# Blocks of many and of few columns by turns, in a three-layer graph attention kernel

## The chip, the cores and the metric

The kernel runs on one core of a Trainium2 chip. The metric is the device time of one execution in microseconds; before the change it is 3365.79 us, the median of three runs (3364.47 to 3366.1). A core has five engines with queues of their own: PE (matrix products), DVE (vector work), ACT (functions and scaling), POOL (here above all the issue of gathers) and SP (plain transfers).

## The reference

There are 6250 nodes with 256 features and 100,000 edges, sorted by destination. Two graph attention layers of 4 heads with 64 features (each with loops from a node to itself) are followed by one of 8 heads with 32 features, with layer normalisation after the second and the third.

```python
# layers 1 and 2 (GATv2): per edge and head
xl = x @ Wl; xr = x @ Wr
logits = sum(leaky_relu(xl[src] + xr[dst], 0.2) * att)      # over a head's features
alpha = exp(logits - max over dst) / sum over dst
out = segment_sum(xl[src] * alpha, dst) + b
# layer 3 (GAT): the logit is a sum of two numbers per node and head
e = leaky_relu(s1[src] + s2[dst], 0.2)
out = segment_sum(softmax over dst (e) * Wh[src], dst)

h = elu(layer1(x)); x = layernorm(x + layer2(h)); x = layernorm(x + layer3(x))
```

Each layer needs, for each node, the rows of all nodes that point to it. A node has 16 such sources on average, some have over 30 and some under 5.

## The kernel before

A planning part (`make_plan`) counts the edges of every node, ranks the nodes by that number, and puts them into 49 blocks of 128, one node to a partition. Block 0 has the nodes with the most edges, block 48 those with the fewest. `columns` gives each block a number of columns, the most edges a node in it may have: 27 in block 0 (edges over that are handled apart, in the `few_...` helpers), then 25, 24, 23, 22, 21, 21, 20, ... down to 10, 10 and 9 in the last ones; 803 in all. While the plan is made the table of layer 1 (rows of x Wl, one to a node) is written to device memory.

`tile_by_degree` then runs the three layers over the blocks, in the order of an instruction stream written out by hand (nothing is rescheduled). For a block with c columns, POOL issues c indirect gathers (L1235), each of which brings one row of about 1 KB to each of the 128 partitions. They go to row tiles of up to 9 rows (`row_tiles`, `chunks`): a block of 28 slots (27 columns and, in layers 1 and 2, the node's own row) takes 4 tiles, 19 to 27 slots take 3, 10 to 18 take 2. There are 9 row tiles, used in turn (`rowp`, L1201); a gather waits until the tile's last user is done.

Layers 1 and 2 are in `layer2`. In iteration b the streams are: POOL `start(b + 3)` (layer 1 only: one gather of the nodes' lists and features) and `gather(b + 1)`; PE and ACT `ready(b + 1)`, the node's own products (layer 1) or copies (layer 2); `attend(b)`: on DVE three passes over each tile (maximum, product with att, sum; L1504 to L1506) for the logits, their maximum (`top`, L1374), on ACT the exponentials (L1381); then `end(b - 1)`, which scales and finishes the block before; DVE's reciprocal of the sum (L1571, called den here, which waits for the exponentials); and `weighted_sum(b)`: DVE multiplies the rows by their weights (L1411), ACT does so for the last few columns (L1410), and PE adds the rows up in PSUM by products with the identity (L1418). Last, the finished row of block b - 1 is transposed (L1355), copied by ACT (xT, L1357), multiplied by the next layer's weights (L1362) and stored by SP: the next layer's table. The block order of PE and ACT is fixed: the transposes of b - 1 stand behind the sums of b, and the exponentials of b + 1 behind the copies of b - 1.

Layer 3 has no products on PE: DVE adds the logits (L1703), weights the rows (L1433) and sums them (L1442); POOL scatters finished rows to the output (L1733).

A layer's gathers need the whole table of the layer before. To begin earlier, `begin` gathers the first columns of the first three blocks (14, 12 and 11, `EARLY`) out of the rows of blocks 0 to 44 only; it stands in POOL's stream behind the last block's gathers. For that, `sort_sources` sorts those blocks' sources in layer 1 (DVE, in `attend` of the following block), so that the early ones lie in these rows.

Of the kernel before, what the change touches and what calls it, by code (L numbers as in the profile page):

```python
# [26 lines left out]
F32 = mybir.dt.float32  # L27
BF16 = mybir.dt.bfloat16
I32 = mybir.dt.int32
AF = mybir.ActivationFunctionType  # L30
OP = mybir.AluOpType
# [4 lines left out]
P = 128  # L36
# [2 lines left out]
EPS = 1e-5  # L39
FAR = 1 << 20  # L40
RUNS = 64
EARLY = (14, 12, 11)
LATE = 4


def columns(E, N, NB):

    mean = E / N
    pmf = [math.exp(-mean)]
    for k in range(1, 200):
        pmf.append(pmf[-1] * mean / k)
    over, sd = [], []
    for c in range(199):
        p = sum(pmf[c + 1 :])
        g = sum((k - mean) * pmf[k] for k in range(c + 1, 200))
        over.append(N * p)  # L60
        sd.append(math.sqrt(max(N * (p * (1.0 - p) - g * g / mean), 0.0)))
    cols = []
    for b in range(NB):
        most = P * b
        cols.append(next(
            c for c in range(199) if (over[c] + 3.5 * sd[c] <= most if b else over[c] < 0.01)
        ))
    low = max((c for c in range(199) if N - over[c] <= P // 4), default=0)
    high = next(c for c in range(199) if over[c] <= P // 4)
    pmf += [0.0] * 200  # L70
    held = next(
        c for c in range(199)
        if N * sum((k - c) * pmf[k] for k in range(c, 200))
        + 3.5 * math.sqrt(N * sum((k - c) ** 2 * pmf[k] for k in range(c, 200))) <= P
    )
    assert cols[1] <= held < cols[0]
    return cols, low, high, held


@with_exitstack  # L80
# [634 lines left out]
def make_plan(  # L715
# [6 lines left out]
    nc = tc.nc  # L722
    N, F = x.shape
    E = src.shape[0]
    NB = node_i.shape[1]
# [12 lines left out]
    one = ctx.enter_context(tc.tile_pool(name="plan_one", bufs=1))  # L738
# [4 lines left out]
    ps = ctx.enter_context(tc.tile_pool(name="plan_ps", bufs=1, space=PSUM))  # L743
# [301 lines left out]
    place_f = one.tile([P, NB], F32, name="place_f")  # L1045
# [3 lines left out]
    piece = one.tile([P, 2, NB], I32, name="piece")  # L1049
    nc.vector.tensor_single_scalar(piece[:, 0, :], place, P - 1, op=OP.bitwise_and)  # L1050
    nc.vector.tensor_single_scalar(piece[:, 1, :], place, 7, op=OP.logical_shift_right)
    nc.vector.tensor_scalar(vals[:, 2, :], count, 255.0, None, op0=OP.min)
    to = one.tile([P, 2, NB], BF16, name="to")
    nc.vector.tensor_copy(to, piece)
# [56 lines left out]
    pb = ps.tile([P, 2], F32, name="pb", tag="ph")  # L1111
# [31 lines left out]
def tile_by_degree(  # L1143
# [3 lines left out]
    nc = tc.nc  # L1147
# [3 lines left out]
    NB = -(-N // P)  # L1151
# [8 lines left out]
    consts = ctx.enter_context(tc.tile_pool(name="deg_consts", bufs=1))  # L1160
# [13 lines left out]
    spots = sources  # L1174


    AHEAD = (NB - LATE) * P
# [16 lines left out]
    lack = consts.tile([P, FEW], F32, name="few_lack")  # L1194
    few_at = consts.tile([P, 2], I32, name="few_at")
    few_row = consts.tile([P, max(W2 + 1, A1)], F32, name="few_row")
    soon = consts.tile([P, len(EARLY), max(EARLY)], I32, name="soon")
    late = consts.tile([P, len(EARLY)], F32, name="late")
    ones = consts.tile([P, P], F32, name="ones_l")
    nc.gpsimd.memset(ones, 1.0)  # L1200
# [29 lines left out]
    def gather_rows(b, rows, cut, own, table, of, width, j0, j1):  # L1230


        for g, (s0, s1) in zip(rows, cut):
            for j in range(max(s0 - own, j0), min(s1 - own, j1)):
                nc.gpsimd.indirect_dma_start(  # L1235
                    out=g[:, j + own - s0, :width], out_offset=None, in_=table,
                    in_offset=source(of, b, j),
                )
# [74 lines left out]
    def row_tiles(b, own):  # L1313
        cut = chunks(cols[b] + own)
        return [rowp.tile([P, T, RW], F32, name="g") for _ in cut], cut

    def begin(own, table, width):

        for b, n in enumerate(EARLY):
            begun[b] = row_tiles(b, own)  # L1320
            gather_rows(b, *begun[b], own, table[:AHEAD], soon, width, 0, n)

    def sort_sources(work, ps, b):

        n = cols[b]
        keys = work.tile([P, CK], F32, name="keys")
        nc.vector.memset(keys, -float(NP << KEY))
        nc.vector.tensor_single_scalar(
            keys[:, :n], spots[:, b, :n], -float(1 << KEY), op=OP.mult
        )  # L1330
        nc.vector.tensor_sub(keys, keys, number)
        order = work.tile([P, CK], F32, name="order")
        for r in range(0, CK, 8):
            nc.vector.max(order[:, r : r + 8], keys)
            if r + 8 < CK:
                nc.vector.match_replace(keys, order[:, r : r + 8], keys, -BIG)
        places = work.tile([P, CK], I32, name="places")
        nc.vector.tensor_single_scalar(places, order, -1.0, op=OP.mult)
        nc.vector.tensor_single_scalar(spots[:, b, :n], places[:, :n], KEY, op=OP.logical_shift_right)
        e = EARLY[b]  # L1340
        nc.vector.tensor_single_scalar(soon[:, b, :e], spots[:, b, :e], AHEAD - 1, op=OP.min)
        nc.vector.tensor_single_scalar(
            late[:, b : b + 1], spots[:, b, e - 1 : e], float(AHEAD), op=OP.is_ge
        )
        if b + 1 == len(EARLY):
            pb = ps.tile([P, b + 1], F32, name="pb", tag="tp")
            nc.tensor.matmul(pb, ones, late, start=True, stop=True)
            bad = work.tile([P, 1], F32, name="bad")
            nc.vector.reduce_sum(bad, pb, axis=AX.X)
            nc.vector.tensor_single_scalar(done, bad, 0.0, op=OP.is_equal)  # L1350
# [115 lines left out]
    def layer2(i, table, of, width, start, own, finish, follow):  # L1466
# [5 lines left out]
        with ExitStack() as es:  # L1472
            zp = es.enter_context(tc.tile_pool(name=f"z{i}", bufs=1))
            work = es.enter_context(tc.tile_pool(name=f"work{i}", bufs=3))
            ps = es.enter_context(tc.tile_pool(name=f"ps{i}", bufs=2, space=PSUM))
# [6 lines left out]
            def gather(b):  # L1482
                first = EARLY[b] if b in begun else 0
                rows, cut = begun.pop(b) if first else row_tiles(b, 1)
                gather_rows(b, rows, cut, 1, table, of, width, first, cols[b])
                if b == 0:
                    gather_few(table, i, width)
                state[b] = [rows, cut]
# [8 lines left out]
            def attend(b):  # L1497
                rows, cut, xr = state.pop(b)
                S = cols[b] + 1
                lg = work.tile([P, CM + 1, H2], F32, name="lg")  # L1500
                for g, (s0, s1) in zip(rows, cut):
                    n = s1 - s0
                    z = zp.tile([P, T, W2], F32, name="z")[:, :n, :]
                    nc.vector.tensor_max(z, g[:, :n, :W2], xr[:, None, :].to_broadcast([P, n, W2]))  # L1504
                    nc.vector.tensor_mul(z, z, at[:, None, :].to_broadcast([P, n, W2]))  # L1505
                    nc.vector.reduce_sum(  # L1506
                        lg[:, s0:s1, :], z.rearrange("p t (h d) -> p t h d", h=H2), axis=AX.X
                    )
                if b == 0:
                    own_r = work.tile([P, W2], F32, name="few_own", bufs=1)  # L1510
                    nc.scalar.copy(own_r, xr)
                    po = pst.tile([P, W2], F32, name="few_r", tag="tp")
                    nc.tensor.matmul(po, node_of, own_r, start=True, stop=True)
                    none(po)
                    z = zp.tile([P, T, W2], F32, name="z")[:, 0, :]
                    nc.vector.tensor_max(z, few_row[:, :W2], po)
                    nc.vector.tensor_mul(z, z, at)
                    few_lg = work.tile([P, H2], F32, name="few_lg", bufs=1)
                    nc.vector.reduce_sum(few_lg, per_head(z, H2), axis=AX.X)
                    few_logits(work, pst, lg, few_lg, H2)  # L1520
                    if i == 0:
                        nc.vector.tensor_copy(few_at[:, 1:], few_row[:, W2 : W2 + 1])
                few = min(S // 3, cut[-1][1] - cut[-1][0] - 1) if b + 1 < NB else 0
                wt, new = weights(work, ps, lg, S if b else S + FEW, H2, few, S)
                while later:
                    later.pop()()
                if i == 0:
                    for g, (s0, s1) in zip(rows, cut):
                        s = max(s0, 1)
                        nc.scalar.copy(spots[:, b, s - 1 : s1 - 1], g[:, s - s0 : s1 - s0, W2])  # L1530
                    if 0 < b <= len(EARLY):
                        sort_sources(work, pst, b - 1)
                return rows, cut, wt, new

# [55 lines left out]
    def none(t):  # L1590

        nc.vector.memset(t.rearrange("p (h d) -> p h d", h=H2)[:, :, D2:], -BIG)
# [86 lines left out]
    with ExitStack() as es:  # L1679
        work = es.enter_context(tc.tile_pool(name="work3", bufs=3))  # L1680
        ps = es.enter_context(tc.tile_pool(name="ps3", bufs=3, space=PSUM))
# [111 lines left out]
```

## Time and profile before

| | us |
|---|---|
| median of the runs | 3365.79 |
| profiled execution | 3880.55 |
| its span, first to last instruction | 3878.7 |
| DVE busy | 2836.2 |
| POOL busy | 2530.5 |
| PE busy | 1481.8 |
| ACT busy | 1091.1 |

The profiled execution is 515 us longer than the runs. Busy times are added up over the whole program; the layers have different limits, so they are read by stretch. The gathers of layer 1 begin at 154.5 us, those of layer 2 that need all rows at 1512.4, those of layer 3 at 2722.4. A POOL gather counts as busy while it is issued (0.95 us), not until its rows have landed. Idle time in a group's line stands ahead of its instructions, with what ended it.

### The profile page before, as it was taken

To read this page: it belongs to the slowest core of one execution; us is meant where nothing else is said; L and a number is where in the kernel's file an instruction comes from. 1 tells how busy PE (TensorE), PEld (TensorE's weight loads), DVE (VectorE), ACT (ScalarE), POOL (GpSimd) and SP (SyncE) were. 2 spreads that over 40 slices of the span, in tenths; PEclk is the share of its full clock that TensorE was granted. 3 is DMA by queue.
4 is the path that set the end of the run, shared out by engine and by line. 5 is a ranking of instruction groups with operands and counts; after the bars stand their busy time and mean duration, and the time that the engine had idled before them with its cause. 6 is when DMAs were issued, how large, how long until landed. Compare 5 with 4: busy or idle time off the path is not lost.

```text
span 3878.7 us, 23608 instructions
## 1 busy us (share of the span) xinstructions
PE 1481.8 (38%) x5130; PEld 1113.8 (29%) x5130; DVE 2836.2 (73%) x2648; ACT 1091.1 (28%) x4176; POOL 2530.5 (65%) x2613
## 2 busy tenths in 40 slices
PE   6324665556667763355544545554000000000000
PEld 5213444434555542343433433443000000000000
DVE  6228988668888876899876988896676565666665
ACT  3113444334445442243433434443000000000000
POOL 6464666666666645666666666664777777777774
PEclk8656877778788886676666677776555555555555
DMA  8532333333434334333433434442343333333332
GB/s 188 109 92 78 98 104 104 100 99 103 105 102 108 104 79 109 100 106 104 112 107 105 111 107 110 109 111 74 101 108 101 96 97 96 97 97 96 97 97 57
DMA packets 196123, 395.60 MB, mean 102 GB/s; under 512 B 63036, under 2 KB 115514, under 8 KB 195956
## 3 DMA queue, kind: packets, MB, share of 16 engines
q0 software_dynamic: 122048, 338.04, 33.2%
q1 hardware_dynamic: 66226, 54.22, 5.1%
q10 hardware_dynamic: 7698, 1.74, 0.4%
q8 instruction: 45, 0.74, 0.1%
q14 instruction: 106, 0.87, 0.1%
HBM read 353.82 MB, written 40.42 MB: 102 GB/s over the span
## 4 chain that ended last, share of the span: by engine, by line
issue 20%; POOL 20%; DVE 13%; PE 10%; another core or an unknown queue 6%; ACT 5%; DMA 1%; DVEq 0%; POOLq 0%; ACTq 0%
POOL g L1235 18%; PE acc L1418 6%; DVE z L1505 4%; DVE z L1504 4%; DVE lg L1506 3%; PE pm L1362 3%; ACT g L1410 2%; ACT wt L1381 2%; DVE g L1411 1%; POOL out L1733 1%; DMA g<-xl_d,near_r 1%; DVE weighted L1433 1%; ACT xT L1357 0%; PE pt L1355 0%
## 5 line engine op out<-in xcount | busy, mean ns | idle before, releaser
L1235 POOL DMA_INDIRECT g<-xl_d,near_r x1569 | 1487.4, 948 | 858.7 <-issue 454.3
L1418 PE MATMUL acc<-g,ident 128*128 128x256 f32 x3408 | 1015.9, 461 | 765.3 <-issue 282.7
L1418 PEld LDWEIGHTS acc<-g,ident 128*128 128x128 f32 x3408 | 774.4, 234 | 1004.2 <-issue 522.3
L1235 POOL DMA_INDIRECT g<-whs_d,near_r x766 | 793.2, 1036 | 284.2 <-issue 250.0
L1410 ACT ACTIVATE g<-g,by 128x64 f32<-128x64 f32 x2056 | 545.1, 337 | 316.1 <-issue 310.8
L1504 DVE TENSOR_TENSOR z<-g,pr 128x1820 f32<-128x1820 f32 (+4 forms) x234 | 497.1, 2125 | 19.1 <-DMA g<-xl_d,near_r 10.0
L1505 DVE TENSOR_TENSOR z<-z,at 128x1820 f32<-128x1820 f32 (+4 forms) x234 | 497.4, 2126 | 8.0
L1506 DVE TENSOR_REDUCE lg<-z 128x28 f32<-128x1820 f32 (+4 forms) x234 | 497.3, 2125 | 8.1
L1442 DVE TENSOR_REDUCE acc_v<-weighted 128x256 f32<-128x4096 f32 (+15 forms) x49 | 343.7, 7014 | 16.5 <-remote 8.3
L1411 DVE TENSOR_TENSOR g<-g,wt 128x1792 f32<-128x1792 f32 (+8 forms) x234 | 348.4, 1505 | 2.9
L1391 ACT ACTIVATE wt<-lg 128x128 f32<-128x128 f32 (+17 forms) x49 | 14.0, 285 | 851.0 <-DVE top L1374 391.5
L1703 DVE TENSOR_TENSOR lg<-g,s_r 128x56 f32<-128x56 f32 (+4 forms) x111 | 22.1, 213 | 315.1 <-DMA g<-whs_d,near_r 272.5
L1357 ACT COPY xT<-pt 128x256 f32<-128x256 f32 x147 | 54.9, 374 | 688.5 <-remote 342.2
L1433 DVE TENSOR_TENSOR weighted<-g,wt 128x1792 f32<-128x1792 f32 (+4 forms) x111 | 226.6, 2056 | 0.1
L1571 DVE RECIPROCAL den<-den 128x4 f32<-128x4 f32 x98 | 17.4, 177 | 212.9 <-ACT wt L1381 165.2
L1381 ACT ACTIVATE wt<-lg,top 128x19 f32<-128x19 f32 (+14 forms) x392 | 116.0, 296 | 190.8 <-DVE lg L1506 74.3
L1362 PE MATMUL pm<-wcat,xT 128*128 128x260 f32 x392 | 136.0, 505 | 56.3 <-ACT xT L1357 49.8
L1362 PE MATMUL pm<-wh_cat,xT 128*128 128x272 f32 x196 | 77.5, 531 | 183.8 <-ACT xT L1357 95.5
L1537 DVE TENSOR_TENSOR h<-acc,den 128x256 f32<-128x256 f32 x98 | 40.7, 416 | 126.2 <-remote 112.8
L1362 PEld LDWEIGHTS pm<-wcat,xT 128*128 128x128 f32 x392 | 94.8, 255 | 90.5 <-ACT xT L1357 64.6
L1362 PEld LDWEIGHTS pm<-wh_cat,xT 128*128 128x128 f32 x196 | 42.8, 242 | 203.0 <-ACT xT L1357 104.7
L1362 PE MATMUL pl<-wcat,xT 128*128 128x260 f32 x196 | 64.0, 455 | 55.5 <-issue 40.4
(232 smaller groups left out, 1548.4 us busy)
## 6 DMA issues: line engine op xcount, KB each, us to landing
g<-xl_d,near_r POOLq DMA_INDIRECT x1569
g<-whs_d,near_r POOLq DMA_INDIRECT x766
whs_d<-row SPq DMA_DIRECT2D x49, 132.0 KB
xl_d<-xl SPq DMA_DIRECT2D x49, 130.0 KB
xl_d<-row SPq DMA_DIRECT2D x49, 130.0 KB
xr_d<-row SPq DMA_DIRECT2D x49, 130.0 KB
two<-xl_d SPq DMA_DIRECT2D x49, 130.0 KB
two<-xr_d SPq DMA_DIRECT2D x49, 130.0 KB
```

The lines of the kernel that those rows point to most:

```text
L1235: nc.gpsimd.indirect_dma_start(out=g[:, j + own - s0, :width], out_offset=None, in_=table, in_offset=source(of, b, j),)
L1357: nc.scalar.copy(xT, pt)
L1362: nc.tensor.matmul(pm, xT[:, c, :], w[:, c, :], start=c == 0, stop=c == 1)
L1381: nc.scalar.activation(wt[:, :, h], lg[:, :S, h], AF.Exp, bias=top[:, h : h + 1], accum_out=den[:, h : h + 1],)
L1410: nc.scalar.mul(g4[:, t, h, :], g4[:, t, h, :], by[:, t - m, h : h + 1])
L1411: nc.vector.tensor_mul(g4[:, :m], g4[:, :m], wt[:, s0 : s0 + m, :].unsqueeze(3).to_broadcast([P, m, H, F // H]),)
L1418: nc.tensor.matmul(acc, ident, g4[:, t], start=s0 + t == 0, stop=s0 + t == S - 1 and not more)
L1433: nc.vector.tensor_mul(prod[:, s0 - base : s1 - base, :].rearrange("p t (h d) -> p t h d", h=H), g[:, :n, :F].rearrange("p t (h d) -> p t ...
L1442: nc.vector.reduce_sum(part, prod[:, : s1 - base, :].rearrange("p s f -> p f s"), axis=AX.X)
L1504: nc.vector.tensor_max(z, g[:, :n, :W2], xr[:, None, :].to_broadcast([P, n, W2]))
L1505: nc.vector.tensor_mul(z, z, at[:, None, :].to_broadcast([P, n, W2]))
L1506: nc.vector.reduce_sum(lg[:, s0:s1, :], z.rearrange("p t (h d) -> p t h d", h=H2), axis=AX.X)
```

## The change

The numbers of columns are dealt out by turns: block 0 keeps 27, block 1 gets the fewest (9), block 2 the next most (25), block 3 the next fewest (10), and so on, so that the sizes meet in the end: ..., 17, 15, 17, 15, 16, 16, 16, 16, 16. The same nodes stay together; only the place of a block changes. The plan computes the place from the rank in three small DVE instructions and rebuilds the number written to the table in a fourth, so tables, lists and output follow the new order in all three layers. The early gathers are 14 columns of block 0 and 12 of block 2, now the two largest, and only those two are sorted. Numbers of gathers, tiles and bytes stay as they were.

```diff
-EARLY = (14, 12, 11)
+EARLY = {0: 14, 2: 12}
...
     assert cols[1] <= held < cols[0]
-    return cols, low, high, held
+    turns = [0] * NB
+    for r, c in enumerate(cols):
+        turns[min(2 * r, 2 * NB - 1 - 2 * r)] = c
+    return turns, low, high, held
...
     nc.vector.tensor_single_scalar(piece[:, 1, :], place, 7, op=OP.logical_shift_right)
+    back = one.tile([P, NB], I32, name="back")
+    nc.vector.tensor_scalar(
+        back, piece[:, 1, :], -2.0, float(2 * NB - 1), op0=OP.mult, op1=OP.add
+    )
+    nc.vector.tensor_single_scalar(piece[:, 1, :], piece[:, 1, :], 2.0, op=OP.mult)
+    nc.vector.tensor_tensor(piece[:, 1, :], piece[:, 1, :], back, op=OP.min)
+    nc.vector.scalar_tensor_tensor(
+        place_f, piece[:, 1, :], float(P), piece[:, 0, :], op0=OP.mult, op1=OP.add
+    )
...
-        for b, n in enumerate(EARLY):
+        for b, n in EARLY.items():
             begun[b] = row_tiles(b, own)
             gather_rows(b, *begun[b], own, table[:AHEAD], soon, width, 0, n)
...
-        e = EARLY[b]
+        e, k = EARLY[b], list(EARLY).index(b)
...
-        if b + 1 == len(EARLY):
-            pb = ps.tile([P, b + 1], F32, name="pb", tag="tp")
+        if b == max(EARLY):
+            pb = ps.tile([P, k + 1], F32, name="pb", tag="tp")
...
-                    if 0 < b <= len(EARLY):
+                    if b - 1 in EARLY:
                         sort_sources(work, pst, b - 1)
```

More of the change, by code (lines that the diff above doesn't have):

```diff
@@ L1196, in tile_by_degree @@
     few_row = consts.tile([P, max(W2 + 1, A1)], F32, name="few_row")
-    soon = consts.tile([P, len(EARLY), max(EARLY)], I32, name="soon")
+    soon = consts.tile([P, 1 + max(EARLY), max(EARLY.values())], I32, name="soon")
     late = consts.tile([P, len(EARLY)], F32, name="late")
@@ L1339, in sort_sources @@
         nc.vector.tensor_single_scalar(spots[:, b, :n], places[:, :n], KEY, op=OP.logical_shift_right)
-        e = EARLY[b]
+        e, k = EARLY[b], list(EARLY).index(b)
         nc.vector.tensor_single_scalar(soon[:, b, :e], spots[:, b, :e], AHEAD - 1, op=OP.min)
         nc.vector.tensor_single_scalar(
-            late[:, b : b + 1], spots[:, b, e - 1 : e], float(AHEAD), op=OP.is_ge
+            late[:, k : k + 1], spots[:, b, e - 1 : e], float(AHEAD), op=OP.is_ge
         )
-        if b + 1 == len(EARLY):
-            pb = ps.tile([P, b + 1], F32, name="pb", tag="tp")
+        if b == max(EARLY):
+            pb = ps.tile([P, k + 1], F32, name="pb", tag="tp")
             nc.tensor.matmul(pb, ones, late, start=True, stop=True)
```

## The prediction

> **What bounds the kernel now.** I read the busy times and slices of the page first, then stretches cut at the three layers, then the groups, and last the timeline of single blocks.
>
> ```profile
> PE 1481.8 (38%) x5130; PEld 1113.8 (29%) x5130; DVE 2836.2 (73%) x2648; ACT 1091.1 (28%) x4176; POOL 2530.5 (65%) x2613
> ...
> DVE  6228988668888876899876988896676565666665
> ```
>
> DVE is the busiest engine, at 0.8 to 0.9 up to slice 27, then at 0.6. The stretches: planning, first layer, second layer, third layer. The columns are busy us and instruction counts of PE, weight loads, DVE, ACT and POOL, then clock and DMA.
>
> ```profile
> 0.00:154.00 154.00, 84.24 (x419) 66.33 (x419) 67.15 (x113) 40.45 (x136) 81.67 (x103) 0.75 0.79 159
> 154.00:1511.00 1357.00, 796.47 (x2699) 588.45 (x2699) 1030.31 (x944) 519.83 (x1983) 841.51 (x888) 0.77 0.37 99
> 1511.00:2722.00 1211.00, 598.39 (x2006) 457.52 (x2006) 1008.54 (x820) 462.79 (x1861) 761.95 (x804) 0.70 0.39 105
> 2722.00:3879.00 1157.00, 2.68 (x6) 1.51 (x6) 730.25 (x772) 67.98 (x197) 845.42 (x819) 0.50 0.35 95
> ```
>
> In layers 1 and 2 DVE works 1030 and 1009 us; in layer 3 only 730 of 1157, and POOL 845. The groups say what DVE waits for there:
>
> ```profile
> L1235 POOL DMA_INDIRECT g<-xl_d,near_r x1569 | 1487.4, 948 | 858.7 <-issue 454.3 <-PE acc L1418 131.1 <-remote 114.9
> ...
> L1703 DVE TENSOR_TENSOR lg<-g,s_r 128x56 f32<-128x56 f32 (+4 forms) x111 | 22.1, 213 | 315.1 <-DMA g<-whs_d,near_r 272.5 <-DMA out<-y,node_i 22.6 <-issue 19.7
> ```
>
> In layer 3 a block is done soon after its last gather: POOL sets the pace. A gather takes 0.95 us plus an issue gap of 0.30, a stride of 1.25. In layers 1 and 2 gathers are ready long before DVE wants them, and DVE sets the pace.
>
> The profiled execution takes 3880.55 us (span 3878.7), the runs 3365.8. The 515 us between are mostly stalls without a releaser, after which instructions start on a grid of 0.7 us. A floor from durations: start of layer 1 at 163.8, DVE 1027.8, waits for its first rows 9.3, end of layer 1 19, DVE 1009.3, end of layer 2 15, then 816 gathers and puts at 1.25 = 1020, and some 24 after the last gather: 3289. With POOL's own floor for layer 1 (852 x 1.25 = 1065) it is 3326, near the runs. So I take the durations and the 1.25 as those of the runs, and the stalls as mostly the profiled execution's.
>
> **The Trainium skill.** "Perfetto Trace Analysis", section "What 'DMA-bound' means": an issuing queue full of DMA slices is bound by descriptor generation. The trace agrees for layer 3: gathers land about 2 us after POOL ends them while the DMA share is 0.35. The same page, section "Optimization Strategy", says that interleaving regimes with different most-contended engines may help; that would speak for alternation, if large blocks were bound by POOL and small ones by DVE. Here a layer-2 block of 25 columns costs POOL 31.3 and DVE 29.4, one of 10 columns 12.5 and 14.0: little to balance, and the 37 early gathers cover it.
>
> **What the alternation meets: the hand-over between blocks.** After den(b), PE adds up the slots of block b while DVE already works on the logits of b+1. But ACT's exponentials of b+1 stand in its queue behind the copy of a transpose (xT), which PE makes only after the sums of b. One such hand-over in layer 2, 12 slots (columns + own row) each, on DVE (first weighting after den, then the next block's top):
>
> ```profile
> 2617.12 1.75 DVE L1411 TENSOR_TENSOR g<-g,wt 128x1536 f32<-128x1536 f32 x1
> ...
> 2630.33 0.24 DVE L1374 TENSOR_REDUCE top<-lg 128x4 f32<-128x48 f32 x1
> ```
>
> The same on ACT: transpose, row copies, then the exponentials.
>
> ```profile
> 2626.53 0.37 ACT L1357 COPY xT<-pt 128x256 f32<-128x256 f32 x1 [3.12 <-PE acc L1418]
> 2628.17 0.38 ACT L1659 COPY row<-pm 128x264 f32<-128x264 f32 x1 [1.27 <-PE pm L1362]
> 2628.45 0.17 ACT L1660 COPY s_r<-pm 128x8 f32<-128x8 f32 x1
> 2628.51 0.40 ACT L1644 COPY pr<-two 128x260 f32<-128x260 f32 x1
> 2630.60 0.28 ACT L1381 ACTIVATE wt<-lg,top 128x12 f32<-128x12 f32 x1 [1.70 <-DVE top L1374]
> ```
>
> And PE's two long sums, of 26 and 25 slots (two passes a slot):
>
> ```profile
> 1594.50 13.55 PE L1418 MATMUL acc<-g,ident 128*128 128x256 f32 x52 [26.32 <-issue]
> ...
> 1623.99 13.73 PE L1418 MATMUL acc<-g,ident 128*128 128x256 f32 x50 [11.74 <-issue]
> ```
>
> ACT is free at 2628.9 and waits 1.7 us for DVE's top: the hand-over is hidden, narrowly. With n slots in b and m in b+1: ACT is free R = 2.2 + 0.53 n + 3.1 after den (0.53 a slot from 13.55 and 13.73 us for 26 and 25 slots; the last term is 4.0 in layer 1, which has more transposes), DVE's top is there after D = 0.29 (n - few) + 0.89 m + 0.8 (few: columns that ACT weights). For 12 and 12: R 11.7, D 13.8; measured 11.9 and 13.6. With equal neighbours D exceeds R for every size here. With unequal ones it doesn't.
>
> **The change part by part.**
> - Large to small. 28 slots then 10: D = 6.4 + 8.9 + 0.8 = 16.1, R = 20.1 in layer 2, 21.0 in layer 1: DVE waits 4.0 and 4.9. 26 then 11: 3.3 and 4.2; 25 then 11: 3.1 and 4.0; 24 then 12: 1.6 and 2.5; 23 then 12: 1.4 and 2.3; 22 then 13 twice 0.3 and 1.2; then only layer 1, under 1.2 each. Sums 14 and 21. Behind the waiting den stand DVE's weighting, the next logits and so PE's next sums. Small to large leaves 10 to 15 us of slack, which no one can use later. In layer 1 the first stall falls where DVE still waits for its first gathers: 16 rather than 21. Bounds: at 0.42 a slot (PE clock above the profile's 0.7 to 0.77) both together give 4, at 0.57 52.
> - Layer ends. The last block has 17 slots instead of 10 in layers 1 and 2; PE's last sum ends 6.5 instead of 4 us after DVE's weighting: 2 x 2.5 = 5.
> - Early gathers. 26 instead of 37 before the last rows. The 37 were free: POOL then stood 29 us waiting for them (the one wait for whs_d<-row). The 11 now come after the rows, where POOL sets the pace in layer 3: 11 x 1.25 = 13.7. If POOL in the runs has no such pause, the old 11 weren't free and this is 0. In layer 2, where DVE sets the pace and the second block needs 9 gathers only, 0.
> - The end. After the last gather DVE has 16 columns to weight and add instead of 9: weighting 0.28 and summing 0.44 us a column, 7 x 0.72 = 5.1.
> - One sort fewer (13 short DVE instructions, 301.14 to 304.12 us): -2.9 in layer 1.
> - Planning: four DVE instructions on 49 columns, about 0.17 us each, behind POOL's 49 list gathers, which last from 40 to 114 us; 45 memsets for 18, 27 x 0.04 = 1 us, ahead of a POOL wait of 17.4 us for DVE. Nothing; 2 us if that cover is gone.
> - Tiles, gathers in all, DVE's columns and SP's stores are the same in number. The nine tiles now hold 3 + 2 + 3: a tile wait still comes 20 us or more ahead of use. Nothing; from -10 (large blocks starved less in layer 2) to +10.
>
> Sum: 16 + 14 + 5 + 13.7 + 5.1 - 2.9 = 51. Against the profiled execution 3880.6 + 51 = 3931; against the median of the runs 3365.8 + 51 = 3417. I say 3415.
>
> **Rivals.**
> 1. The hand-over stays hidden (PE nearer 0.42 a slot): only the third layer pays, 13.7 + 5.1, with 4 + 5 - 2.9: 3391. For it: PE's duration varies with the clock. Against: the long sums ran at 0.52 and 0.55.
> 2. Faster: DVE in layer 3 has a floor per block, whatever its columns. The last blocks show it:
>
> ```profile
> 3816.08 0.30 DVE L1703 TENSOR_TENSOR lg<-g,s_r 128x40 f32<-128x40 f32 x2
> ...
> 3835.95 0.30 DVE L1703 TENSOR_TENSOR lg<-g,s_r 128x40 f32<-128x40 f32 x2
> ```
> From block 43 on each takes 20 to 21 us for 10 busy, and DVE ends 24 us behind POOL. A floor of 21 in the runs would bind wherever 1.25 (c + 1) is below it, in the 22 blocks under 16 columns, 79 us in all; a pair of the new order takes POOL 43 and the floor 42, so all of it is gained: 51 - 79 = -28, 3338. At 20 us the gain is 57 and it decides from there on. Against: blocks 37 and 41 took 17.9 and 17.4 us and still waited for gathers, and the rebuilt total leaves no room for it.
> 3. No change: the stalls of layer 1 and 2 fall on DVE waits that the runs have anyway (those unplaced 40 us), and the 11 gathers weren't free: 51 - 30 - 13.7 = 7, 3373.
>
> **Numbers.** Forecast 0.60; rival 1 0.13, rival 2 0.20, rival 3 0.07. A difference of 0.2% (7 us) is about what a measurement of this kernel can tell from no change. So slower 0.60 + 0.13 = 0.73, same 0.07, faster 0.20. The likeliest case's own range is 3390 (0.45 a slot) to 3450 (0.57, and PE late by 2 us at some large-to-small steps, as in the trace). The range over all is 3342 to 3450: the upper end holds the bounds of the stalls, the lower reaches to rival 2.
>
> **What would show it.** In the profile after: den L1571 waiting for ACT wt 4 to 6 us in every second of the first dozen blocks of layers 1 and 2, and near 0 between; DVE's busy time within 5 us of 2836; 13 + 9 + 13 gathers after the rows at the start of layer 3, and its last gather some 14 us later after the rows than now; 5 us more from the last gather to the end. Wrong would make it: small blocks in layer 3 that took 20 us before and cost nothing now (rival 2), large-to-small steps without a wait (rival 1), or a POOL that is starved of tiles.

## The result: 3407.4 us after 3365.9, 1.2% slower

The changed kernel takes 3407.43 us (median of four runs, 3406.76 to 3408.42) beside 3365.94 us for the kernel before; the ratio is 1.0121, 95% interval 1.0105 to 1.0137. The forecast was 3415 with a range of 3342 to 3450: 49 us more were foretold, 41.5 came.

The profile of the kernel before that the prediction read (span 3878.7 us) is not of an execution like the timed ones, most likely because it ran on a slow chip (last section); run again, the same code left a profile with a span of 3366.3 us, as long as the timed runs. From here "before" in a trace is that second profile, called desc_again, and it is compared with the profile of the changed kernel (span 3405.7).

The busy times and slices of the changed kernel's page:

```profile
PE 1333.9 (39%) x5130; PEld 1064.7 (31%) x5130; DVE 2836.0 (83%) x2635; ACT 1043.5 (31%) x4160; POOL 2464.8 (72%) x2640
...
DVE  7388999999999988899999999995976666666666
```

DVE works exactly as long as before (2836.0). Nothing was made costlier; all of the loss is waiting. Where it lies is seen when both spans are cut at the same four events: the first logits of layers 1, 2 and 3, and the end of the last gather. The columns are as in the prediction. The changed kernel, then desc_again:

```profile
141.10:1260.80 1119.70, 690.31 (x2682) 551.51 (x2680) 1025.71 (x914) 483.00 (x1972) 823.80 (x869) 0.82 0.44 117
1260.80:2366.40 1105.60, 559.05 (x2008) 445.29 (x2008) 1009.33 (x824) 451.38 (x1852) 777.49 (x822) 0.74 0.43 117
2366.40:3379.80 1013.40, 1.95 (x4) 1.00 (x4) 714.38 (x750) 65.52 (x190) 768.14 (x806) 0.50 0.40 107
3379.80:3405.70 25.90, 0.00 (x0) 0.00 (x0) 15.98 (x19) 2.47 (x7) 4.33 (x8) 0.50 0.08 28
```

```profile
139.70:1250.60 1110.90, 702.61 (x2682) 560.27 (x2681) 1027.51 (x931) 485.80 (x1980) 835.94 (x880) 0.82 0.44 120
1250.60:2344.10 1093.50, 560.73 (x2008) 446.26 (x2008) 1008.67 (x824) 453.79 (x1860) 778.62 (x822) 0.73 0.43 118
2344.10:3344.70 1000.60, 1.95 (x4) 1.01 (x4) 718.73 (x751) 65.58 (x190) 758.65 (x795) 0.50 0.39 107
3344.70:3366.30 21.60, 0.00 (x0) 0.00 (x0) 11.07 (x19) 2.43 (x7) 4.33 (x7) 0.50 0.11 34
```

| stretch | before | after | more | foretold |
|---|---|---|---|---|
| to the first logits | 139.7 | 141.1 | 1.4 | 0 |
| layer 1 | 1110.9 | 1119.7 | 8.8 | 16 + 2.5 - 2.9 = 15.6 |
| layer 2 | 1093.5 | 1105.6 | 12.1 | 14 + 2.5 = 16.5 |
| layer 3 to the last gather | 1000.6 | 1013.4 | 12.8 | 13.7 |
| after the last gather | 21.6 | 25.9 | 4.3 | 5.1 |
| sum | 3366.3 | 3405.7 | 39.4 | 51 |

The four stretches for which a change was foretold moved that way, each by less than foretold. In layer 3 POOL has 806 instructions for 795: the 11 gathers.

**The hand-over in the trace.** DVE's waits in the first third of layer 1 (190 to 700 us), before and then in a second run of the changed kernel (after_again, below), with total, times and longest wait in us:

```profile
DVE den L1571 <- ACT wt L1381: 11.3, 16, 0.7
DVE bad L1349 <- PE pb L1347: 0.7, 1, 0.7
```

```profile
DVE den L1583 <- ACT wt L1393: 22.6, 20, 3.8
DVE bad L1361 <- PE pb L1359: 3.2, 1, 3.2
```

Single blocks of the changed kernel, den of blocks 2, 4, 5, 6, 7 and 8 in layer 1 (the odd ones have 10 or 11 columns and follow a large block):

```profile
237.92 0.18 DVE L1583 RECIPROCAL den<-den 128x4 f32<-128x4 f32 x1 [0.76 <-ACT wt L1393]
288.64 0.18 DVE L1583 RECIPROCAL den<-den 128x4 f32<-128x4 f32 x1 [0.75 <-ACT wt L1393]
310.12 0.18 DVE L1583 RECIPROCAL den<-den 128x4 f32<-128x4 f32 x1 [3.77 <-ACT wt L1393]
336.64 0.18 DVE L1583 RECIPROCAL den<-den 128x4 f32<-128x4 f32 x1 [0.75 <-ACT wt L1393]
357.59 0.18 DVE L1583 RECIPROCAL den<-den 128x4 f32<-128x4 f32 x1 [3.22 <-ACT wt L1393]
383.16 0.18 DVE L1583 RECIPROCAL den<-den 128x4 f32<-128x4 f32 x1 [0.74 <-ACT wt L1393]
```

A wait of 0.7 is the time of the exponentials themselves, which every block of layer 1 has. The 3 us above it are the hand-over. (Block 3 has no wait at den: DVE has by then waited 3.1 us for the result of the sorts, `bad`, which PE makes behind the sums of block 2.) The step from 24 to 10 columns in layer 2 shows each link, PE and ACT:

```profile
1397.62 13.63 PE L1430 MATMUL acc<-g,ident 128*128 128x256 f32 x50 [17.99 <-DVE sd L1473]
1411.08 0.38 PE L1367 MATMUL pt<-ident,near_r 128*128 128x128 f32 x2
```

```profile
1411.50 0.37 ACT L1369 COPY xT<-pt 128x256 f32<-128x256 f32 x1 [5.68 <-PE pt L1367]
1413.14 0.38 ACT L1671 COPY row<-pm 128x264 f32<-128x264 f32 x1 [1.27 <-PE pm L1374]
...
1413.79 0.30 ACT L1393 ACTIVATE wt<-lg,top 128x11 f32<-128x11 f32 x1
```

and DVE, the first line the end of the logits, the last the wait:

```profile
1410.04 0.23 DVE L1386 TENSOR_REDUCE top<-lg 128x4 f32<-128x44 f32 x1
1411.28 0.42 DVE L1549 TENSOR_TENSOR h<-acc,den 128x256 f32<-128x256 f32 x1 [1.01 <-PE acc L1430]
...
1415.54 0.18 DVE L1583 RECIPROCAL den<-den 128x4 f32<-128x4 f32 x1 [2.70 <-ACT wt L1393]
```

The maximum is there at 1410.3, the exponentials start only at 1413.8, because ACT sat 5.7 us ahead of the xT copy, which waited for 13.6 us of sums (25 slots at 0.55). The chain of waits tells the same: "PE acc" has 4% of desc_again's chain and 7% of the changed kernel's.

### The profile page after: what moved, and what is told of

It is laid out like the page before. It is cut to its first block, busy times and chain, and to the rows that moved or that the text cites. A ratio compares the mean times of both kernels' runs of the same rounds, so it can differ in the third digit from the quotient of the medians.

```text
span 3405.7 us, 23633 instructions
## 1 busy us (share of the span) xinstructions
PE 1333.9 (39%) x5130; PEld 1064.7 (31%) x5130; DVE 2836.0 (83%) x2635; ACT 1043.5 (31%) x4160; POOL 2464.8 (72%) x2640
## 4 chain that ended last, share of the span: by engine, by line
DVE 30%; POOL 28%; issue 19%; PE 7%; DMA 6%; ACT 3%; DVEq 0%; POOLq 0%; ACTq 0%
POOL g L1247 27%; DVE z L1517 8%; DVE z L1516 8%; DVE lg L1518 8%; PE acc L1430 7%; DMA g<-xl_d,near_r 4%; ACT wt L1393 2%; DVE g L1423 2%; DMA g<-whs_d,near_r 1%; DVE weighted L1445 1%; POOL out L1745 1%; DVE top L1386 1%; DMA out<-y,node_i 1%; PE pm L1374 0%; DMA near_r<-near_d,node_i 0%
## 5 line engine op out<-in xcount | busy, mean ns | idle before, releaser
L1430 PE MATMUL acc<-g,ident 128*128 128x256 f32 x3408 | 957.2, 450 | 817.6 <-DVE sd L1473 466.2
L1247 POOL DMA_INDIRECT g<-whs_d,near_r x777 | 737.9, 950 | 271.4 <-issue 228.2
L1422 ACT ACTIVATE g<-g,by 128x64 f32<-128x64 f32 x2040 | 496.2, 334 | 0.0
L1393 ACT ACTIVATE wt<-lg,top 128x18 f32<-128x18 f32 (+14 forms) x392 | 115.5, 295 | 503.8 <-DVE top L1386 486.0
L1403 ACT ACTIVATE wt<-lg 128x112 f32<-128x112 f32 (+17 forms) x49 | 14.0, 285 | 815.5 <-DVE lg L1402 815.5
L1374 PE MATMUL pm<-wcat,xT 128*128 128x260 f32 x392 | 99.0, 396 | 22.6 <-ACT xT L1369 22.6
L1374 PEld LDWEIGHTS pm<-wcat,xT 128*128 128x128 f32 x392 | 70.4, 189 | 42.8 <-ACT xT L1369 34.2
L1001 POOL DMA_INDIRECT near<-list_d,begin_i x49 | 60.0, 1224 | 31.1 <-DVE begin_i L996 16.5
L1393 ACT ACTIVATION_READ_ACCUMULATOR wt<-lg,top 128x1 f32 x392 | 73.3, 187 | 0.0
L1745 POOL DMA_INDIRECT out<-y,node_i x49 | 49.8, 1017 | 30.2 <-ACT y L1476 16.0
```

The source lines that it names most:

```text
L1247: nc.gpsimd.indirect_dma_start(out=g[:, j + own - s0, :width], out_offset=None, in_=table, in_offset=source(of, b, j),)
L1374: nc.tensor.matmul(pm, xT[:, c, :], w[:, c, :], start=c == 0, stop=c == 1)
L1393: nc.scalar.activation(wt[:, :, h], lg[:, :S, h], AF.Exp, bias=top[:, h : h + 1], accum_out=den[:, h : h + 1],)
L1422: nc.scalar.mul(g4[:, t, h, :], g4[:, t, h, :], by[:, t - m, h : h + 1])
L1430: nc.tensor.matmul(acc, ident, g4[:, t], start=s0 + t == 0, stop=s0 + t == S - 1 and not more)
L1745: put = nc.gpsimd.indirect_dma_start(out=out[:, :], out_offset=node(b), in_=y, in_offset=None, bounds_check=N - 1, oob_is_err=False,)
```

## The experiments

A ratio is to the kernel before on the same chip. Three chips were used: the kernel before took 3366.9 us on the first, 3883.9 on the second (here "the slow chip") and 3372.3 on the third.

**desc_again: the kernel before once more**, nothing edited, for its profile.

> The kernel before once more, for a profiled execution of the length of the runs. Theory (hand-over, end of layers, fewer early gathers): its span is near 3364, the DVE waits between the blocks of layers 1 and 2 are about 1 us a block, POOL has the pause of about 30 us ahead of the late gathers of layer 3, and the blocks 43 to 48 of layer 3 take 12 to 16 us each, not 20 to 21. Rival (a floor of 20 us for a small block in layer 3): the last blocks take 20 to 21 us here too.

Measured: 3365.99 us (ratio 0.9996, interval 0.9987 to 1.0005), span 3366.3. DVE idles 0.7 to 1.2 us in most blocks of layers 1 and 2, as expected. Blocks 43 to 48 of layer 3 take 17.0, 13.5, 16.0, 12.5, 17.1 and, to the end, 18.7 us, some more than the 12 to 16 expected; but rival 2's floor of 20 us is not there. It was in the first profile alone. One expectation failed: POOL has no pause of 30 us ahead of the late gathers of layer 3. Its early gathers end at 2321.9 and the late ones begin at 2322.7:

```profile
L1235 POOL DMA_INDIRECT g<-whs_d,soon x37: 942/947/954, 2275.9 to 2321.0; - x37
L1235 POOL DMA_INDIRECT g<-whs_d,near_r x6: 942/946/947, 2322.7 to 2328.9; - x6
```

**desc_26: fewer early gathers in the old order.**

```diff
-EARLY = (14, 12, 11)
+EARLY = (14, 12)
```

> The order of before, with 14 and 12 early gathers for its first two blocks and none for the third (one sort fewer). Theory: 11 gathers more at POOL's pace at the start of layer 3, 11 x 1.25 = 13.7, less 2.9 for the sort: 3366 + 11 = 3377, and nothing in layer 2. Rival (the 11 early gathers were not free): 3363 to 3366.

Measured: 3379.68 us, 12.8 more than before (11 expected, the sort counted), ratio 1.0039 (1.0025 to 1.0053). The theory holds, its rival falls. In the trace layer 3 takes 1014.2 us from its first logits to its last gather, for 1000.6: 13.6 more, against 11 x 1.25 = 13.7. Its 26 early gathers end at 2305.2, and the late ones still begin only at 2320.0, 2.7 us earlier than with 37:

```profile
L1235 POOL DMA_INDIRECT g<-whs_d,soon x26: 942/947/954, 2272.9 to 2304.2; - x26
L1235 POOL DMA_INDIRECT g<-whs_d,near_r x8: 942/946/949, 2320.0 to 2328.8; - x8
```

**desc_end16: the last block has 16 columns, the order is else the old one.** Ranks 24 and 48 exchange places, 37 early gathers as before.

```diff
+    turns = list(cols)
+    turns[NB // 2], turns[NB - 1] = cols[NB - 1], cols[NB // 2]
```

> The order of before, with the blocks of 16 and of 9 columns at places 24 and 48 exchanged; early gathers as before. Theory: 5.1 us more after the last gather of layer 3 and 2.5 us more at the end of each of layers 1 and 2: 3366 + 10 = 3376. Rival (the ends of layers 1 and 2 hide under the late gathers, or POOL stands waiting anyway): 3366 + 5 = 3371. Rival (the end of a layer costs nothing): 3366.

Measured: 3379.20 us, 12.3 more, ratio 1.0039 (1.0025 to 1.0053): near the 10 that were foretold, but not all from the places that were foretold. After the last gather the trace has 25.9 us for 21.6 (4.3 more). Layer 1 is 3.8 and layer 2 is 2.5 us longer, but about 2 of each is the new step from 16 to 9 columns in the middle: that block's DVE idle time is 2.9 us in both layers where its neighbours have 1.0 and 0.7. That leaves 1.9 us for the end of layer 1 and 0.3 for that of layer 2, where 2.5 each were foretold.

**shift: turns with small steps.** Rank r goes to place 2r, and ranks from 25 on to 2r - 49: 27, 16, 25, 16, 24, 15, ..., 16, 9, 16.

```diff
-        turns[min(2 * r, 2 * NB - 1 - 2 * r)] = c
+        turns[2 * r - (NB if 2 * r > NB else 0)] = c
```

> Large and small blocks by turns, but with steps down of 7 to 11 columns only: 27, 16, 25, 16, 24, 15, 23, 15, ..., 10, 16, 9, 16. Early gathers (14 of block 0, 12 of block 2), the last block of 16 columns and the turns themselves are as in the changed kernel. Theory (the exponentials of a small block wait for the sums of the large one ahead of it): by the formula the first steps down leave no wait and only the last ones wait, 2 us in layer 2 and 7 in layer 1; against 22 us of such waits in the trace of the changed kernel that makes 3407 - 22 + 6 = 3391. Rival (the turns cost by themselves, by tiles that come free late or by fewer gathers ahead): 3407.

Measured: 3400.39 us, ratio 1.0099 (1.0083 to 1.0114). The gain on the changed kernel, which did not run on this chip, is about 7 us by the two ratios (their intervals overlap a little; the traces differ by 5.5), not 16. The waits lie where the formula puts them. DVE in layer 1, first the blocks before 1030 us, then those after, with total, times and longest:

```profile
DVE den L1584 <- ACT wt L1394: 24.8, 35, 0.9
```

```profile
DVE den L1584 <- ACT wt L1394: 14.8, 10, 3.3
```

Up to the step from 17 to 12 columns no wait is over 0.9; from the step from 17 to 11 on every small block waits longer, up to 3.3. So alternation itself costs nothing, and a step down from 25 to 16 is free. But the late steps cost 8 us in layer 1 and 6 in layer 2 above the ordinary wait, where 6.6 and 2.1 come out of the formula: for blocks of 9 to 11 columns it is up to 1.4 us too kind. In the worst of them, the step from 16 to 9 in layer 2, PE's 17 slots take 0.62 us each, where 0.53 was taken over from two sums of 25 and 26 slots; 17 x 0.09 is 1.5 us:

```profile
2283.26 10.52 PE L1431 MATMUL acc<-g,ident 128*128 128x256 f32 x34 [10.64 <-DVE sd L1474]
```

The gain lies in layer 2 alone, 1100.3 us for 1105.6. Layer 1 takes 1119.9 for 1119.7: DVE idles 3.3 us less between its first and last block, and 3.8 us more in those two.

**turns_37, and turns_37_b: the changed kernel with 37 early gathers.**

```diff
-EARLY = {0: 14, 2: 12}
+EARLY = {0: 20, 2: 17}
```

> The changed kernel with 20 and 17 early gathers for the blocks of 27 and 25 columns in place of 14 and 12, so 37 in all as before the change. Theory (fewer early gathers cost POOL's pace in layer 3, and in the changed kernel POOL stands 35 us ahead of the late ones): 3407 - 11 x 1.25 = 3393; nothing in layer 2, where DVE sets the pace. Rival (the pause ends later too, or the early rows of the changed order come later): 3400 or more.

On the slow chip: 3953.30 us, ratio 1.0188 (1.0165 to 1.0211). The changed kernel has no time on that chip, so this decides nothing; the same kernel stands beside it on the third chip, as turns_37_b.

> The changed kernel with 20 and 17 early gathers, again, to be held against the changed kernel on the same chip. Theory: 13.7 less than the changed kernel, in layer 3 alone. Rival (a later start of the late gathers takes it back): no difference, or more.

**after_again: the changed kernel itself**, nothing edited, beside its variants.

> The changed kernel itself, so that its variants have it beside them on one chip: chips differ, the kernel before takes 3366 on some and 3884 on another. Where before takes 3366: 3407. Where before takes 3884: theory (the chip adds stalls to every engine in nearly the same number, the change costs the same 41): 3925; rival (small blocks behind large ones make the stalls of such a chip worse): 3940 or more.

Measured: 3414.38 us, ratio 1.0123 (1.0108 to 1.0139), as at first. turns_37_b took 3403.66 us, ratio 1.0091 (1.0076 to 1.0107): 10.7 less than the changed kernel beside it, where 13.7 was foretold. POOL's waits from 2350 us to the end, after_again, then turns_37_b:

```profile
POOL g L1247 <- DMA whs_d<-row: 35.0, 1, 35.0
POOL out L1745 <- ACT y L1476: 16.0, 2, 10.5
```

```profile
POOL g L1247 <- DMA whs_d<-row: 21.2, 1, 21.2
POOL out L1745 <- ACT y L1476: 19.4, 3, 10.5
```

The pause ahead of the late gathers shrinks by 13.8 us, which is the 11 gathers. Then 3.4 us are given back: POOL is now so far ahead in the first blocks that its scatter of a finished block waits for DVE. The theory holds, less that wait.

**turns_front, and turns_front_b: the transposes ahead of the sums.** In the changed kernel, one order on PE and ACT is turned round: the transposes, products and copies of block b - 1 now stand ahead of the sums of block b.

```diff
                     if b:
-                        last.append(rest())
+                        rest()()
...
-                if last:
-                    last[0]()
```

> The changed kernel with the transposes of block b - 1, its products with the next weights and ACT's copies of them ordered ahead of the sums of block b on PE, instead of behind them. The same work, one order changed. Theory (the waits at steps from a large to a small block come from the exponentials standing behind a copy that stands behind the sums): the 22 us of such waits in the trace go, but for some 3 us that DVE then waits for the sums themselves: 3407 - 19 = 3388. Rival (the waits are of another kind, such as tiles or gathers that come late): 3403 to 3410.

On the slow chip: 3892.98 us, ratio 1.0023 (1.0011 to 1.0034), again with no time of the changed kernel to hold it against.

> The changed kernel with the transposes ahead of the sums, again, to be held against the changed kernel on the same chip. Theory: 19 less than the changed kernel, with the waits of den at the steps from 25 to 10 and the like gone from the trace. Rival: no difference.

Measured: 3417.70 us, ratio 1.0133 (1.0118 to 1.0149), 3.3 more than the changed kernel. The expectation of 19 less failed. DVE's waits in the first third of layer 2 (1320 to 1700 us), after_again, then turns_front_b:

```profile
DVE den L1583 <- ACT wt L1393: 14.9, 17, 2.7
DVE h L1549 <- PE acc L1430: 2.0, 2, 1.1
```

```profile
DVE h L1549 <- PE acc L1430: 10.6, 6, 3.3
DVE den L1583 <- ACT wt L1393: 4.1, 11, 0.4
```

The waits of den did go (2.7 at the longest to 0.4), so the exponentials did stand behind that copy. Most of them, 8.6 of 10.8 us, came back a few instructions earlier, at `h<-acc`, which needs the sums themselves. In the step from 24 to 10 the sums now start behind the transposes and products of the block before:

```profile
1406.32 2.18 PE L1374 MATMUL pm<-wh_cat,xT 128*128 128x272 f32 x4 [0.46 <-ACT xT L1369]
1408.29 12.23 PE L1430 MATMUL acc<-g,ident 128*128 128x256 f32 x50
```

and end at 1420.5, 3.3 us after DVE's maximum; in the changed kernel `h<-acc` already waited 1.0 us there. So DVE had two limits close together, and the copy was only the later one. What holds a small block up is that PE must finish a large block within the time of the small block's logits; whichever part of PE's work stands last, DVE waits for it.

That explains why little was gained, not why 3.3 us were lost. Between the first and last blocks DVE idles 0.7 us less in layer 1 and 2.4 less in layer 2. The loss lies mostly at the ends of the layers, where DVE idles 3.9 us more in the first and last block of layer 1 and 1.6 more in those of layer 2: the last block has no next logits to cover its sums, and they too now stand behind the products of the block before. At the end of layer 1 (1225 to 1275 us), after_again, then turns_front_b:

```profile
DVE h L1549 <- PE acc L1430: 6.5, 1, 6.5
```

```profile
DVE h L1549 <- PE acc L1430: 10.8, 1, 10.8
```

**desc_front: the same reordering in the old order.**

> The kernel before with the same reordering on PE and ACT as the run with the transposes ahead of the sums. Theory (with equal neighbours the hand-over is hidden): within 4 us of 3366. Rival (the reordering is worth something by itself, by rows stored earlier at the ends of layers or otherwise): 3350 to 3360.

On the slow chip: 3864.56 us, ratio 0.9945 (0.9926 to 0.9964), 19 us less. The theory gave its 4 us for a chip where the kernel before takes 3366, so this neither holds nor fails it; why it gains on the slow chip stays open.

**desc_49_late5: more early gathers, begun earlier, in the old order.**

```diff
-EARLY = (14, 12, 11)
-LATE = 4
+EARLY = (17, 17, 15)
+LATE = 5
```

> The order of before, with 17, 17 and 15 early gathers in place of 14, 12 and 11, taken out of the rows of blocks 0 to 43 instead of 0 to 44, so that they can begin a block earlier. Theory: in the order of before the 37 gathers end just as the last row lands (a pause of 0.4 us), so 12 more pay only if they begin earlier; POOL stood 17.5 us ahead of them, which is room for 12 x 1.25 = 15: 3366 - 15 = 3351. Rival (tiles, not the row of block 44, hold the early gathers back): 3360 to 3366.

On the slow chip: 3840.18 us, ratio 0.9882 (0.9863 to 0.9902), 44 us less. On that chip there is a pause ahead of the late gathers, 22.7 us in desc_front's trace (29.0 in the first profile); here 14.5 us of it are left, so the 12 gathers fitted in. They are worth 15 us (12 x 1.25); where the rest of the 44 comes from stays open.

**desc_49_front: both of these edits.**

> The order of before, with 49 early gathers out of the rows of blocks 0 to 43 and the transposes ahead of the sums. Theory: where before takes 3366, 15 less for the gathers and 0 to 4 for the reordering: 3347 to 3351; where before takes 3884, the two ratios of the single runs together, 0.9882 x 0.9945 = 0.983: 3817. Rival (the two gain the same time, an earlier last row): no more than one of them alone.

On the third chip: 3367.85 us, ratio 0.9985 (0.9978 to 0.9991). It is faster than both kernels, but faster than the one before by 4.5 us only, and not by 15. Neither edit was run alone on such a chip, so what each is worth there is not shown. POOL's early gathers ahead of layer 2 and ahead of layer 3, with first and last start:

```profile
L1235 POOL DMA_INDIRECT g<-xl_d,soon x49: 942/949/1007, 1203.5 to 1263.8; - x49
```

```profile
L1235 POOL DMA_INDIRECT g<-whs_d,soon x49: 942/949/1105, 2272.2 to 2332.5; - x49
L1235 POOL DMA_INDIRECT g<-whs_d,near_r x8: 945/947/949, 2335.5 to 2344.3; - x8
```

Ahead of layer 3 the early gathers work: from the first late gather to the last one ends POOL takes 1008.7 us for 1022.0 in desc_again, 13.3 less. Ahead of layer 2 they harm. POOL is busy with layer 1 until 1203.2, so 49 early gathers last until 1264.7, while DVE starts layer 2 at 1256.2; DVE then waits 4.9 us for the late rows of block 0 (0.3 in desc_again). From first logits to first logits layer 1 is 1.0 and layer 2 3.6 us longer than in desc_again, and layer 3 up to its last gather 9.7 shorter. One number of early gathers serves two boundaries with different room. About 37 for the first and 49 for the second, where POOL still waits 2.1 us for the last rows, would fit these traces; that was not run.

## Why the prediction was right, and where its sizes were off

- **Large to small, in place and kind right.** The formula gave 4.0 and 3.1 us for the step from 24 to 10 in layers 1 and 2; above the ordinary idle time of such a block (1.0 and 0.7) the trace has 3.8 and 3.3. For 23 to 11 it gave 2.5 and 1.6; the trace has 2.5 and 1.1. A slot cost 0.55 us in the step shown, for 0.53 assumed. But the sum over a layer was too large: DVE's idle time outside the first and last block rose by 12.6 us in layer 1 (16 foretold, 48.8 to 61.4) and 10.8 in layer 2 (14 foretold, 34.6 to 45.4).
- **The terms that failed inside it.** In layer 2 it is the first step, 27 to 9: it was to cost 4.0 us and costs nothing. The other steps there were to cost 10, and came to 10.8. Block 0 has the edges beyond 27, and DVE waits for PE's sums of that block anyway, in the changed kernel as before (11.1 us). The line is from DVE's waits in the changed kernel from 1255 to 1312 us, the start of layer 2:

```profile
DVE few_weight L1315 <- PE few_w L1310: 10.1, 1, 10.1
```

When DVE begins with block 1, PE is done with block 0. Nor does any block stand before block 0 whose row would have to be transposed and copied ahead of the exponentials of block 1. In layer 1 the prediction had left the first step out, for the wait for the first gathers. There the steps down from 25, from 22 and twice from 21 were mis-sized: 4.2, 2.3, 1.2 and 1.2 us were foretold, 2.8, 1.2, 0.3 and 0.5 came. Why is not shown.

- **Layer ends, 5 us foretold.** PE's last sums do end later after DVE: `h<-acc` waits 6.5 us for 4.6 at the end of layer 1, 8.1 for 5.1 at the end of layer 2, near what was foretold (with the old order it also took 5.8 and 6.3, in desc_26, so a single trace is good to about 1 us here). But what followed had slack: DVE's first logits of layer 2 then waited 0.8 us for ACT instead of 2.9, and layer 3's wait for `few_row` fell from 27.5 to 25.9. The last block's idle time changed by -0.1 us in layer 1 and +1.5 in layer 2, the first block's by -1.8 and -0.8: together -2.0 and +0.7. The step that failed is "2 x 2.5 = 5": a later end was counted without asking which waits behind it would shrink.
- **One sort fewer, -2.9.** DVE's busy time in layer 1 fell by 1.8 us. But the result of the sorts is added up on PE behind the sums of block 2, a large block, and DVE waits 3.1 us for it where it waited 0.7; it is the hand-over again, in the place of den's wait in block 3, and is counted in the 12.6. That the wait was moved next to a large block was not seen.
- **Early gathers, 13.7: about right, but for a wrong reason.** The runs show 12.8 (desc_26) and 10.7 (turns_37_b). The prediction read a pause of 29 us in its profile and wrote that, were it absent in the runs, "the old 11 weren't free and this is 0". It is absent there, and by its own words this term would be 0; that it came out near 13.7 is luck. The old 11 were free all the same: POOL waits ahead of the early gathers instead (17.5 us in desc_again), and the 37 end 0.8 us ahead of the late ones. Without the 11 POOL stands still until 2320.0 (desc_26), 2.7 us earlier than with them, and the layers before end 2.3 us earlier there.
- **After the last gather, 5.1:** measured 4.3. **Planning, 0:** 1.4 between these two profiles; after_again began its first logits 5.8 us later than the first profile of the same kernel, on a chip where the kernel before takes 6 us more, so 1.4 is no finding.
- **The profile itself.** The prediction put the 515 us between profile and runs down to the profiled execution. Timed runs of the slow chip take as long, so they are most likely not the profiler's but the chip's. That it worked with durations and left these stalls out is what kept its sizes near.
- **Rivals.** The hand-over is not hidden (rival 1, 3391), and no long sum of the changed kernel's layers 1 and 2 took the 0.42 us a slot that it needs (0.45 at the least); no floor of 20 us for a block in layer 3 exists in the trace of desc_again (rival 2, 3338); and the waits of layers 1 and 2 did not fall on waits that were there anyway, but for block 0 and the layer ends (rival 3, 3373).

The measured sum, 12.6 - 1.8 - 2.0 = 8.8 for layer 1, 10.8 + 0.6 + 0.7 = 12.1 for layer 2 (idle time between the first and last block, DVE's busy time, idle time of those two), 12.8, 4.3 and 1.4, is 39.4, against 41.5 between the medians.

## What to carry to other kernels

Where two engines hand blocks to each other with a depth of one, unequal neighbours lose on each step down that is too large (25 to 10 here, not 25 to 16) what no step up gives back; compare the second engine's time for block b with the first one's for block b + 1, per pair, and not the sums. Reordering the queue between them helps only if the place that is cleared was the later limit by far: look at the next wait behind the one that is to go, and at the ends, where no next block covers it. And work that is done while an engine must wait for a last row is worth just as much as the pause has room for, which is to be measured at each boundary, on the chip that is timed.

## What the runs showed of the hardware that was not expected

Chips differ by more than any edit here. The kernel before takes 3366.9, 3372.3 and 3883.9 us on three chips (each seen once, so it may also be a state that the slow one was in), and the edits are worth different amounts: 49 early gathers 44 us on the slow one, and, with the reordering, 4.5 on another. Which chip the first profile came from is not known. But its 3880.55 us lie among the 27 runs of the kernel before on the slow chip (3868.5 to 3900.3), and its granted clock of 0.665 among those of the four profiles from there (0.658 to 0.669; 0.686 to 0.695 in all others). In that profile DVE's work is as long as in desc_again (2836.2 us for 2836.0), and so are the gathers of layers 1 and 2 (948 ns for 949). PE is busy longer (1481.8 us for 1349.0), and so is a gather of layer 3 (1036 ns for 950). Above all, instructions start late with no releaser. ACT's weighting of rows, the first profile, then desc_again:

```profile
L1410 ACT ACTIVATE g<-g,by 128x64 f32<-128x64 f32 x2056 | 545.1, 337 | 316.1 <-issue 310.8 <-DMA g<-xl_d,near_r 4.2
```

```profile
L1410 ACT ACTIVATE g<-g,by 128x64 f32<-128x64 f32 x2056 | 500.0, 334 | 0.0
```

What makes that chip so was not found, nor what the change costs on it.

The order of PE's work also changed how long each piece took. These are PE's sums and products around the step from 24 to 10 columns in layer 2, with the granted clock behind the counts. In the changed kernel the sums come first:

```profile
1397.60:1411.25 13.65, 13.63 (x52) 0.81 0.24 66
1411.90:1413.10 1.20, 1.18 (x4) 1.00 0.35 76
```

In turns_front_b the products do:

```profile
1406.30:1408.30 2.00, 1.98 (x5) 0.50 0.40 94
1408.30:1420.50 12.20, 12.20 (x51) 0.89 0.38 102
```

In both, the piece that comes first has the lower clock, and the same four products take 2.2 us for 1.2. So one figure for a slot, such as the 0.53 of the prediction, does not hold for every order and size of block.
